# A decoder layer: the feed forward in three bfloat16 planes behind a survey of its weights, and score sets read by two engines

## The chip, the cores and the metric

The kernel runs on one core of a Trainium2 chip. The time is device microseconds of one execution; the lower the better. The number to predict is the median of the timed runs of the changed kernel, to be set beside 1361.11 us, the median of three runs of the kernel before (1361.1 to 1364.54 us).

A core has five engines that matter here, each with its own stream of instructions, executed in order, and semaphores between them: TensorE (PE, with its weight loads shown apart as PEld), VectorE (DVE), ScalarE (ACT), GpSimd (POOL) and SyncE (SP), which issues most of the DMAs. Matmul results land in PSUM, in eight banks of 512 float32 columns by 128 partitions.

## The reference

A decoder layer in float32: causal self-attention, cross-attention to 77 context rows, and a gated feed forward with two further hidden layers, each with a residual and a layer norm behind it. B = 2, T = 1024, C = 256, 16 heads of 16, hidden size 1024.

```python
def _L0_ffn_ref(x, w1_w, w1_s, w2_w, w2_s, h1_w, h1_s, h2_w, h2_s, w3_w, w3_s):
    h = jax.nn.silu(_tlin(x, w1_w, w1_s)) * _tlin(x, w2_w, w2_s)
    h = jax.nn.gelu(_tlin(h, h1_w, h1_s), approximate=False)
    h = jax.nn.gelu(_tlin(h, h2_w, h2_s), approximate=False)
    return _tlin(h, w3_w, w3_s)
...
x = _layernorm(x + _L0_attn_ref(x, L0_attn_w_qkv, L0_attn_w_proj), axis=-1)
x = _layernorm(x + _L0_xattn_ref(x, ctx_1024, ctx_1024, mask, ...), axis=-1)
x = _layernorm(x + _L0_ffn_ref(x, ...), axis=-1)
```

`_tlin(x, w, s)` is `x @ w.T * s`. The five feed-forward matrices hold only -8, 0 and 8 (ternary values times 8); the scales `s` are ordinary float32 vectors. In bfloat16 a weight of -8, 0 or 8 is the same number as in float32.

## The kernel before

The 16 tiles of 128 tokens are worked on in five chunks, `CHUNKS = ((0, 0, 2), (0, 2, 2), (1, 0, 4), (0, 4, 4), (1, 4, 4))`, each (batch, first tile, tiles). For a chunk the stages are, by the names of the code:

- `start` / `project`: transpose the tokens, project to queries, keys and values, rotate, and pad each head to 32 rows (`qk_pads`, two buffers). Keys and values live in blocks of four tiles, `kT` and `v`, from a pool of three.
- `top` / `maxima` (L353): for each query tile and each span of keys, a set of scores for four heads goes into `su`, the one tile of four PSUM banks (`ps_u`, one buffer). VectorE reads the whole set, up to 2048 columns, and reduces it to `part`. The maximum is then written into the query, so that the next stage subtracts it in the matmul itself.
- `weighted` / `values` (L388 to L416): for each group of four heads and each key tile, scores into the same `su`, one exponential by ScalarE over all four banks into `pr` (L400), a triangular mask by GpSimd on the diagonal (L403), and the product with the values into `po` one step later.
- `rest`: `self_finish` (divide, project, residual, norm) and `cross` (the same scheme with the context's keys: maxima at L461, exponentials at L482).
- `fed` / `feed_forward`: from the normalized tokens, transposed in `transposed_tokens`, the gated pair `pg`, `pu` (8 pairs, two matmuls each), two hidden layers `pf` (8 x 8 matmuls each), and the last matrix (8 matmuls a tile). All are float32. Weights come in 22 slices of 128 x 1024, each fetched anew for every chunk by SP into a pool of five (`wffn`).

What sets the order. `run(start(0))`, `top(0)`, `weighted(0)`, `cross_keys()` come first, then `rest(0)` together with `start(1)`. From there `beside(work, filler)` runs: the attention of the chunks 1 to 4 is the work, the feed forward of chunks that have left attention is the filler. Each `yield` of the attention gives a number of microseconds as credit, and so much feed forward is put in; `filling` ties a feed-forward matmul to the attention two steps back (`AHEAD = 2`), so that it does not run further ahead. What is left of the feed forward when the attention ends runs alone (the tail). `alone` marks the last chunk, where the hidden layers' Gelu reads PSUM directly instead of four at a time. Within this the scheduler of the program orders the instructions of each engine.

Most matmuls are issued in two helpers, so in the profile attention's are at L69 and the feed forward's at L83.

Of the kernel before, what the change touches and what calls it, by code (L numbers as in the profile page):

```python
# [10 lines left out]
U8 = mybir.dt.uint8  # L11
AF = mybir.ActivationFunctionType
# [4 lines left out]
P = 128  # L17
# [10 lines left out]
CHUNKS = ((0, 0, 2), (0, 2, 2), (1, 0, 4), (0, 4, 4), (1, 4, 4))  # L28
# [8 lines left out]
def kernel(ctx: ExitStack, tc: tile.TileContext, a: dict, out: bass.AP):  # L37
# [7 lines left out]
    small = pool("small", 4)  # L45
    wself = pool("wself")
    wcross = pool("wcross")
    keys = pool("keys", 3)
    queries = pool("queries", 2)
    work = pool("work", 2)  # L50
    probs = pool("probs", 2)
    ps_u = ctx.enter_context(tc.tile_pool(name="ps_u", bufs=1, space=PSUM))
    ps_o = ctx.enter_context(tc.tile_pool(name="ps_o", bufs=1, space=PSUM))
    ps_f = ctx.enter_context(tc.tile_pool(name="ps_f", bufs=3, space=PSUM))
# [32 lines left out]
    def bank(name="pm"):  # L87
        return ps_f.tile([P, 512], F32, tag="f", name=name)

    def scores_bank(name="su"):  # L90
        return ps_u.tile([P, 4, 512], F32, tag="u", name=name)
# [31 lines left out]
    for i in range(2):  # L123
        pad = wself.tile([P, 2, H, 32], F32, name=f"qk_pad{i}")
        nc.gpsimd.memset(pad, 0.0)
        nc.gpsimd.memset(pad[:, 1, :, D : D + 1], -1.0)
        qk_pads.append(pad)
# [7 lines left out]
    bv = wcross.tile([1, C], F32, name="bv")  # L135
# [5 lines left out]
    maskk = wcross.tile([L, T], BF16, name="maskk")  # L141
    kx = [wcross.tile([P, NG, L], F32, name=f"kx_{b}") for b in range(B)]
# [9 lines left out]
    def cross_keys():  # L152

        with ExitStack() as first:
# [6 lines left out]
            nc.sync.dma_start(wv, a["wvT"].rearrange("(k p) n -> p k n", p=P))  # L161
            for w, name in ((bk, "bk"), (bv, "bv"), (bq, "bq"), (bo, "bo")):
                nc.sync.dma_start(w, a[name])
# [33 lines left out]
    def add_residual(xt, ps, mv):  # L197

        nc.vector.tensor_tensor(xt, ps, xt, ALU.add)
        stats = small.tile([P, 6], F32, tag="stats", name="stats")  # L200
        nc.vector.bn_stats(stats, xt)
        nc.vector.bn_aggr(mv, stats)

    def normalize(tiles, mv):
        rstd = small.tile([P, len(tiles)], F32, tag="rstd", name="rstd")
# [5 lines left out]
    def transposed_tokens(b, t0, n):  # L211

        xT = work.tile([P, KC, n * P], F32, tag="xTc", name="xTc")
# [17 lines left out]
    def attend(osb, i):  # L231
# [5 lines left out]
        rec = small.tile([P, H, 1], F32, tag="rec", name="rec")  # L237
        nc.vector.reciprocal(rec, pov[:, :, D : D + 1])
        y = work.tile([P, C], F32, tag="y", name="y")
# [7 lines left out]
        yT = work.tile([P, KC, P], F32, tag="yT", name="yT")  # L247
# [5 lines left out]


    kT, v = {}, {}

    def project(b, t0, n, q):

        kb = t0 // KT
        if t0 % KT == 0:  # L260
            kT[b, kb] = keys.tile([P, NG, KB], F32, tag="kT", name="kT")
            v[b, kb] = keys.tile([P, KT, H * DV + 16], F32, tag="v", name="v")
            nc.gpsimd.memset(v[b, kb], 1.0)
        for i in range(n):
# [4 lines left out]
            xT = work.tile([P, KC, P], F32, tag="xT", name="xT")  # L269
# [6 lines left out]
            turned = work.tile([P, 2, H, D], F32, tag="turned", name="turned", bufs=1)  # L276
# [8 lines left out]
            pad = qk_pads[i % 2]  # L285
# [9 lines left out]
            nc.scalar.copy(heads_of(v[b, kb][:, t % KT])[:, :, :D], pv[:, :C].rearrange("p (h d) -> p h d", h=H))  # L295
            yield 0.3
            for s, to, at in ((0, q, i), (1, kT[b, kb], t % KT)):
# [22 lines left out]
    def maxima(b, t0, n, q):  # L320

        for i in range(n):
            cols = slice(i * P, (i + 1) * P)
            spans = spans_of(t0 + i)
            part = small.tile([P, len(spans), NG, 4], F32, tag="part", name="part")
            for m, (kk, c0, c1) in enumerate(spans):
# [3 lines left out]
                for g0 in range(0, NG, gs):  # L330
# [8 lines left out]
                    for gi in range(gm):  # L339
                        for j in range(4):  # L340
# [6 lines left out]
                                        kT[b, kk][rows, g0 + gi, c0:c1],  # L347
# [5 lines left out]
                    nc.vector.tensor_reduce(  # L353
                        part[:, m, g0 : g0 + gm, :].rearrange("p g j -> p j g"),
                        su[:, :, : gm * r].rearrange("p j (g r) -> p j g r", g=gm),
                        AX.X,
                        ALU.max,
                    )
                    yield 2.6 * gm * r / KB
# [4 lines left out]
    def values(b, t0, n, q, osb):  # L364

        nk = t0 + n
        for g in range(NG):
            po = ps_o.tile([P, n * P], F32, tag="o", name="po")

            def weigh(k, q0, pr):  # L370
# [4 lines left out]
                            values_of(v[b, k // KT][:, k % KT], 4 * g + j),  # L375
# [8 lines left out]
            for k in range(nk):  # L384
# [7 lines left out]
                            kT[b, k // KT][rows[j], g, k % KT * P : (k % KT + 1) * P],  # L392
# [6 lines left out]
                pr = probs.tile([P, 4, n * P], F32, tag="pr", name="pr")  # L399
                nc.scalar.activation(pr[:, :, q0:], su[:, :, q0 : n * P], AF.Exp)  # L400
# [14 lines left out]
                yield 1.4 * (n * P - q0) / KB  # L415
# [4 lines left out]
    def self_finish(b, t0, n, osb):  # L420
        mv = small.tile([P, n, 2], F32, tag="mv", name="mv")
# [11 lines left out]
    def cross(b, t0, n):  # L433
        x1T = yield from transposed_tokens(b, t0, n)
        qx = queries.tile([P, NG, n * P], F32, tag="q", name="qx")
# [6 lines left out]
        for i in range(n):  # L442
# [7 lines left out]
            for g in range(NG):  # L450
# [9 lines left out]
            top = small.tile([P, NG, 4], F32, tag="top", name="top")  # L460
            nc.vector.tensor_reduce(  # L461
                top.rearrange("p g j -> p j g"),
                su[:, :, : NG * L].rearrange("p j (g l) -> p j g l", g=NG),
                AX.X,
                ALU.max,
            )
# [4 lines left out]
            yield 2.0  # L471
        osb = work.tile([P, NG, n * P], F32, tag="osb", name="osb", bufs=1)
        for g in range(NG):
# [7 lines left out]
            pr = probs.tile([P, 4, n * P], F32, tag="pr", name="pr")  # L481
            nc.scalar.activation(pr[:L], su[:L, :, : n * P], AF.Exp)  # L482
            po = ps_o.tile([P, n * P], F32, tag="o", name="po")
# [8 lines left out]
            yield 1.4 * n / KT  # L492
        mv = small.tile([P, n, 2], F32, tag="mv", name="mv")
# [12 lines left out]
    def feed_forward(b, t0, n, alone):  # L506


        slices = iter(range(N12 + 2 * NH + N3))

        def weights():
            w = wffn.tile([P, SLICE], F32, tag="wf", name="wf")
            nc.sync.dma_start(w, a["wf"][next(slices)])
            return w

        x2T = yield from transposed_tokens(b, t0, n)
        hid = acts.tile([P, FC, n * P], F32, tag="hid", name="hid")
        for f in range(FC):
            if f % 2 == 0:
                w = weights().rearrange("p (f s k n) -> p f s k n", f=2, s=2, k=KC)  # L520
            pg = bank("pg")[:, : n * P]
            for k in range(KC):
                filling(pg, w[:, f % 2, 0, k, :], x2T[:, k, :], start=(k == 0), stop=(k == KC - 1))
            yield 0.43 * n
            pu = bank("pu")[:, : n * P]
            for k in range(KC):
                filling(pu, w[:, f % 2, 1, k, :], x2T[:, k, :], start=(k == 0), stop=(k == KC - 1))

            gate = acts.tile([P, n * P], F32, tag="gate", name="gate", bufs=2)
            nc.scalar.activation(gate, pg, AF.Tanh, scale=sc[:, 0, f : f + 1])  # L530
            nc.vector.scalar_tensor_tensor(gate, gate, 1.0, pg, ALU.add, ALU.mult)
            nc.vector.scalar_tensor_tensor(hid[:, f, :], pu, sc[:, 1, f : f + 1], gate, ALU.mult, ALU.mult)
            yield 0.43 * n
        for s in (2, 3):
            nxt = acts.tile([P, FC, n * P], F32, tag="hid" if s == 3 else "mid", name="nxt")
            for f in range(FC):
                w = weights().rearrange("p (k n) -> p k n", k=FC)
# [5 lines left out]
                if alone:  # L543
# [71 lines left out]
    def top(n):  # L615
        yield from maxima(*CHUNKS[n], q[n])

# [127 lines left out]
```

## Time and profile before

| what | value |
|---|---|
| median of three runs | 1361.11 us |
| the profiled execution | 1359.41 us |
| its span, first to last instruction | 1357.7 us |
| mean granted TensorE clock | 0.932 |
| instructions in the span | 15205 |
| moved by DMA | 66.19 MB, mean 49 GB/s |
| feed-forward weight slices | 110 DMAs of 512 KB, median 3.2 us to landing |

A page's rows of groups give the line, the engine, the operation, what it writes and reads with its shape, the count, then busy us and mean ns of one, then the idle time of the engine just before such instructions and what ended it. A float32 matmul appears as two MATMUL records. Matmuls are pipelined and the record of one spans its way through the array, so the records of a run overlap: the cost of one in a run is the distance from start to start, not its own length. In the timeline a run of equal instructions is merged into one row: start, length from the first start to the last end, and the count.

The page's chain that ended last gives TensorE 82% of the span, ScalarE 7%, VectorE 7%.

### The profile page before, as it was taken

What the parts mean: (1) busy time and instruction counts of PE and PEld (TensorE: products, weight loads), DVE (VectorE), ACT (ScalarE), POOL (GpSimd) and SP (SyncE); (2) the same over time, 40 slices, a digit from 0 to 9 for tenths busy, and PEclk for the clock granted to TensorE, in tenths of its full rate; (3) what the DMA queues carried; (4) which work ended last, traced back from release to release, by engine and by line L of the source; (5) the groups of instructions that cost most, each with busy time, mean ns of one, the idle gap of its engine ahead of it and who ended that gap; (6) DMA issues with size and microseconds to landing.
All of it is one profiled execution on the core that took longest, in us unless ns stands there. A gap on an engine that the chain in (4) does not pass through costs nothing.

```text
span 1357.7 us, 15205 instructions
## 1 busy us (share of the span) xinstructions
PE 1245.1 (92%) x6672; PEld 638.9 (47%) x6672; DVE 455.4 (34%) x705; ACT 304.9 (22%) x328; POOL 84.0 (6%) x131
## 2 busy tenths in 40 slices
PE   6978998898999999998989999899899798999997
PEld 3554646675466755432225544543222343554445
DVE  3133603346133347750003334686000232140002
ACT  1211151211431121004452212010444303011110
POOL 2110011000211000000011000000000000000000
PEclk7585899898899899999999989899899998999999
DMA  5010211122111112110000000111000000122220
GB/s 161 32 47 0 78 48 47 48 78 85 47 61 49 63 47 70 47 63 16 32 31 17 31 31 32 47 47 47 32 31 17 32 26 22 62 92 72 73 74 15
DMA packets 24594, 66.19 MB, mean 49 GB/s; under 512 B 4328, under 2 KB 9553, under 8 KB 24529
## 3 DMA queue, kind: packets, MB, share of 16 engines
q1 hardware_dynamic: 24257, 64.44, 14.3%
q8 instruction: 52, 0.85, 0.3%
q10 hardware_dynamic: 272, 0.79, 0.2%
q14 instruction: 13, 0.11, 0.0%
HBM read 63.12 MB, written 2.10 MB: 48 GB/s over the span
## 4 chain that ended last, share of the span: by engine, by line
PE 82%; ACT 7%; DVE 7%; POOL 2%; issue 2%; DMA 1%; SPq 0%; POOLq 0%; ACTq 0%; DVEq 0%
PE pf L83 36%; PE su L69 18%; PE pm L69 7%; PE po L69 6%; PE pg L83 4%; PE pu L83 4%; ACT pr L400 3%; DVE part L353 2%; PE pq L69 2%; PE pt L226 1%; ACT pr L482 1%; PE pt L235 1%; PE pt L300 1%; DVE top L461 1%; PE pt L246 1%
## 5 line engine op out<-in xcount | busy, mean ns | idle before, releaser
L83 PE MATMUL pf<-nxt,wf 128*128 128x512 f32 (+1 forms) x640 | 251.1, 535 | 0.0
L83 PE MATMUL pf<-hid,wf 128*128 128x512 f32 (+1 forms) x640 | 249.8, 524 | 0.0
L353 DVE TENSOR_REDUCE part<-su 128x4 f32<-128x2048 f32 (+3 forms) x76 | 165.5, 2178 | 76.2 <-PE su L69 75.8
L400 ACT ACTIVATE pr<-su 128x2048 f32<-128x2048 f32 (+1 forms) x104 | 140.6, 1352 | 208.9 <-PE su L69 208.7
L83 PEld LDWEIGHTS pf<-hid,wf 128*128 128x128 f32 x640 | 113.4, 190 | 119.8 <-issue 114.3
L83 PEld LDWEIGHTS pf<-nxt,wf 128*128 128x128 f32 x640 | 122.0, 201 | 98.5 <-issue 91.1
L69 PE MATMUL su<-q,kT 17*128 17x512 f32 (+3 forms) x832 | 97.7, 538 | 26.7 <-ACT pr L400 24.8
L69 PE MATMUL su<-kT,q 16*128 16x128 f32 (+3 forms) x1152 | 92.3, 434 | 12.4 <-DVE part L353 12.1
L546 DVE TENSOR_SCALAR nxt<-pf,sc 128x256 f32<-128x256 f32 (+1 forms) x64 | 39.4, 615 | 181.6 <-PE pf L83 181.0
L69 PE MATMUL po<-pr,v 128*32 128x512 f32 (+3 forms) x832 | 90.5, 510 | 2.0 <-POOL pr L403 1.5
L69 PEld LDWEIGHTS su<-q,kT 17*128 17x128 f32 x832 | 35.6, 197 | 90.1 <-ACT pr L400 59.1
L417 DVE COPY osb<-po 128x512 f32<-128x512 f32 (+1 forms) x20 | 11.7, 585 | 186.7 <-PE po L69 186.7
L403 POOL TENSOR_SCALAR_AFFINE_SELECT pr<-pr 128x512 f32<-128x512 f32 x64 | 40.6, 635 | 513.6 <-ACT pr L400 513.6
L69 PEld LDWEIGHTS su<-kT,q 16*128 16x128 f32 x1152 | 45.7, 205 | 51.9 <-DVE part L353 25.9
L83 PE MATMUL pg<-xTc,wf 128*128 128x512 f32 (+1 forms) x160 | 69.2, 552 | 0.3 <-DVE xTc L218 0.3
L83 PE MATMUL pu<-xTc,wf 128*128 128x512 f32 (+1 forms) x160 | 65.8, 530 | 0.1
L530 ACT ACTIVATE gate<-pg,sc 128x512 f32<-128x512 f32 (+1 forms) x40 | 24.1, 601 | 185.2 <-PE pg L83 185.1
L83 PE MATMUL pf<-wf,nxt 128*128 128x256 f32 x256 | 58.4, 385 | 0.0
L548 ACT ACTIVATE nxt<-nxt 128x1024 f32<-128x1024 f32 (+1 forms) x16 | 23.7, 1483 | 134.1 <-DVE nxt L546 133.9
L83 PEld LDWEIGHTS pf<-wf,nxt 128*128 128x128 f32 x256 | 48.7, 193 | 9.0 <-issue 1.6
L565 DVE TENSOR_TENSOR o<-pf,s 128x256 f32<-128x256 f32 x16 | 6.8, 423 | 134.8 <-PE pf L83 134.8
L482 ACT ACTIVATE pr<-su 77x2048 f32<-77x2048 f32 (+1 forms) x20 | 30.6, 1531 | 64.2 <-PE su L69 64.2
(103 smaller groups left out, 1018.9 us busy)
## 6 DMA issues: line engine op xcount, KB each, us to landing
wf<-in_wf_dram SPq DMA_DIRECT2D x110, 512.0 KB, 3.2
x<-in_x_dram SPq DMA_DIRECT2D x16, 128.0 KB, 3.4
out_dram<-x SPq DMA_DIRECT2D x16, 128.0 KB, 1.8
wqkv<-in_w_qkv_dram ACTq DMA_DIRECT2D x1, 768.0 KB, 4.9
wk<-in_wkT_dram SPq DMA_DIRECT2D x1, 512.0 KB, 5.2
wq<-in_wqT_dram SPq DMA_DIRECT2D x1, 512.0 KB, 3.5
rope<-in_rope_dram SPq DMA_DIRECT2D x1, 256.0 KB, 5.1
wproj<-in_w_proj_dram SPq DMA_DIRECT2D x1, 256.0 KB, 5.0
```

The lines of the kernel that those rows point to most:

```text
L69: latest[0] = nc.tensor.matmul(*args, **kw).ins
L83: ins = nc.tensor.matmul(*args, **kw).ins
L226: nc.tensor.transpose(pt[:, g * P : (g + 1) * P], m_pad[:, 4 * g : 4 * g + 4, :].rearrange("p h d -> p (h d)"), ident)
L235: nc.tensor.transpose(pt[:, g * P : (g + 1) * P], osb[:, g, i * P : (i + 1) * P], ident)
L246: nc.tensor.transpose(pt[:, k * P : (k + 1) * P], y[:, k * P : (k + 1) * P], ident)
L353: nc.vector.tensor_reduce(part[:, m, g0 : g0 + gm, :].rearrange("p g j -> p j g"), su[:, :, : gm * r].rearrange("p j (g r) -> p j g r", g=gm),
L400: nc.scalar.activation(pr[:, :, q0:], su[:, :, q0 : n * P], AF.Exp)
L403: nc.gpsimd.affine_select(out=pr[:, :, q0 : q0 + P], in_=pr[:, :, q0 : q0 + P], compare_op=ALU.is_ge, fill=0.0, base=0, pattern=[[0, 4], [ ...
L482: nc.scalar.activation(pr[:L], su[:L, :, : n * P], AF.Exp)
L530: nc.scalar.activation(gate, pg, AF.Tanh, scale=sc[:, 0, f : f + 1])
L546: nc.vector.tensor_scalar(nxt[:, f, :], pf, sc[:, s, f : f + 1], None, ALU.mult)
L548: nc.scalar.activation(nxt[:, f - 3 : f + 1, :], nxt[:, f - 3 : f + 1, :], AF.Gelu)
```

## The change

1. **A survey and a branch.** While chunk 0 is in attention, `survey` reads the 22 weight slices once. VectorE takes the maximum of the low halves of the 32-bit words, ScalarE copies the high halves as bfloat16, and a DMA writes that copy to `wh` in DRAM. One matmul adds the partitions' maxima up; `flag` is 0 if all low halves are zero. All engines load the flag and branch. `start(0)` is followed by chunk 0's attention, the cross keys, the remaining loads, `rest(0)` and `start(1)` beside the survey; everything from `top(1)` on is built twice, once in each arm.
2. **Three planes.** In the arm for flag 0 the activation is split: `upper` is the high half of the float32 word as bfloat16, the remainder is taken by VectorE, its high half is `mid`, and what is left is stored as bfloat16 in the low halves, `lower`. Each matmul becomes three bfloat16 products, one for each plane, with float32 sums in PSUM. `upper` and `lower` are read in place, at a step of two bfloat16 elements. The other arm is the float32 feed forward.
3. **Two banks each.** In `largest` ScalarE copies banks 2 and 3 of a score set to `aside` while VectorE reduces banks 0 and 1; VectorE then reduces the copy. In `exponentials` VectorE copies banks 2 and 3 to `pr` while ScalarE takes the exponential of banks 0 and 1; ScalarE then does the copied half in place.
4. **Buffers, order, pace.** Keys and values have two fixed blocks, queries two fixed buffers (the cross queries reuse a chunk's own), `qk_pads` one. The chunk (0, 4, 4) comes before (1, 0, 4). Credits: 1.6 instead of 2.6 for a maximum, 0.6 instead of 1.4 for an exponential, 1.3 instead of 2.0 for a cross maximum; a feed-forward step counts 0.215 us a product of 512 columns.

```diff
-CHUNKS = ((0, 0, 2), (0, 2, 2), (1, 0, 4), (0, 4, 4), (1, 4, 4))
+CHUNKS = ((0, 0, 2), (0, 2, 2), (0, 4, 4), (1, 0, 4), (1, 4, 4))
...
+    def largest(to, su):
...
+        nc.scalar.copy(aside, su[:, 2:])
+        nc.vector.tensor_reduce(to[:, :2], su[:, :2], AX.X, ALU.max)
+        nc.vector.tensor_reduce(to[:, 2:], aside, AX.X, ALU.max)
+
+    def exponentials(pr, su):
+
+        nc.vector.tensor_copy(pr[:, 2:], su[:, 2:])
+        nc.scalar.activation(pr[:, :2], su[:, :2], AF.Exp)
+        nc.scalar.activation(pr[:, 2:], pr[:, 2:], AF.Exp)
...
-                    nc.vector.tensor_reduce(
+                    largest(
                         part[:, m, g0 : g0 + gm, :].rearrange("p g j -> p j g"),
                         su[:, :, : gm * r].rearrange("p j (g r) -> p j g r", g=gm),
-                        AX.X,
-                        ALU.max,
                     )
-                    yield 2.6 * gm * r / KB
+                    yield 1.6 * gm * r / KB
...
-                nc.scalar.activation(pr[:, :, q0:], su[:, :, q0 : n * P], AF.Exp)
+                exponentials(pr[:, :, q0:], su[:, :, q0 : n * P])
...
-                yield 1.4 * (n * P - q0) / KB
+                yield 0.6 * (n * P - q0) / KB
...
+    def split(x, mid, k0, k1):
+
+        upper, lower = word_halves(x)
+        left = pl.acts.tile([P, k1 - k0, x.shape[-1]], F32, tag="left", name="left", bufs=2)
+        nc.vector.tensor_tensor(left, x[:, k0:k1, :], upper[:, k0:k1, :], ALU.subtract)
+        left_upper = word_halves(left)[0]
+        nc.scalar.copy(mid[:, k0:k1, :], left_upper)
+        nc.vector.tensor_tensor(lower[:, k0:k1, :], left, left_upper, ALU.subtract)
+
+    def planes_summed(sums, K, step, first):
...
+        if first:
+            early = K // 2 if K > KC else 0
+            runs = [[(p, k) for k in range(early) for p in range(3)]] if early else []
+            runs += [[(p, k) for k in range(early, K)] for p in range(3)]
+        else:
+            runs = [[(p, k) for k in range(K) for p in range(3)]]
...
+                    filling(
+                        ps,
+                        *operands(p, k),
...
+    def survey(flag):
...
+            for i in range(N12 + 2 * NH + N3):
+                w = raw.tile([P, SLICE], F32, tag="w", name="w")
+                nc.sync.dma_start(w, a["wf"][i])
+                low = w.bitcast(U16).rearrange("p (n two) -> p n two", two=2)[..., 0]
+                nc.vector.tensor_reduce(seen[:, i : i + 1], low, AX.X, ALU.max)
+                h = raw.tile([P, SLICE], BF16, tag="h", name="h")
+                nc.scalar.copy(h, w.bitcast(BF16).rearrange("p (n two) -> p n two", two=2)[..., 1])
+                nc.sync.dma_start(wh[i], h)
+                yield 1
...
+    with part():
+        run(start(0))
+        run(together((chain(top(0), weighted(0), cross_keys(), attention()), 1.0), (survey(flag), 0.8)))
+    other_weights = nc.values_load(flag, min_val=0, max_val=1)
...
+    with tc.If(other_weights == 0) as exact:
+        beside_each_other(feed_forward_exact, 5)
+    with exact.Else():
+        beside_each_other(feed_forward, 4)
```

The new `feed_forward_exact` has the loops of `feed_forward`. The first sums of a layer are made in pairs, in the order of `first` above, so that the planes that are ready late are used late; `split` is called for every two blocks of a finished hidden layer.

## The prediction

> **What bounds the kernel now.** I read the page first, then busy time by stretches, then the timeline where one kind of work stands alone, then the waits.
>
> ```profile
> PE 1245.1 (92%) x6672; PEld 638.9 (47%) x6672; DVE 455.4 (34%) x705; ACT 304.9 (22%) x328; POOL 84.0 (6%) x131
> ```
>
> TensorE is busy nearly throughout, the others a third or less. Cutting the span where the kinds of work change (first feed-forward matmul at 142 us, last attention matmul at 1162) gives, with busy us and instruction counts:
>
> ```profile
> 0.00:142.00 142.00, 109.67 (x672) 64.01 (x672) 45.22 (x79) 22.89 (x43) 17.06 (x36) 0.67 0.18 57
> 142.00:1162.00 1020.00, 947.82 (x5499) 479.80 (x5496) 378.06 (x558) 263.64 (x260) 63.13 (x89) 0.96 0.13 44
> 1162.00:1358.00 196.00, 187.61 (x506) 95.06 (x505) 32.15 (x69) 18.41 (x25) 3.77 (x6) 0.99 0.20 67
> ```
>
> Columns after the width: PE, weight load, DVE, ACT, POOL, granted clock, DMA share, GB/s. The opening has no filler: attention of chunk 0 runs as a chain of latencies at clock 0.67. The middle is attention with feed forward between its sets, the tail feed forward alone. In both TensorE is the bound, so what counts is the price of one pass:
>
> ```profile
> 1289.63 6.60 PE L83 MATMUL pf<-nxt,wf 128*128 128x512 f32 x15
> 1290.06 0.19 PEld L83 LDWEIGHTS pf<-nxt,wf 128*128 128x128 f32 x1 [0.24 <-issue]
> 1290.49 0.19 PEld L83 LDWEIGHTS pf<-nxt,wf 128*128 128x128 f32 x1 [0.24 <-issue]
> ```
>
> ```profile
> 1183.32 2.97 PE L83 MATMUL pf<-wf,nxt 128*128 128x256 f32 x13
> ```
>
> ```profile
> 307.50 1.03 PE L69 MATMUL su<-causal,ident_h 128*128 128x512 bf16 x4
> ```
>
> Weight loads start 0.43 us apart, so a float32 pass over 512 columns costs 0.43; the counts (640 records for 320 matmuls) say two passes a matmul, 0.86. At 256 columns (2.97-0.38)/12 = 0.216. The last record of a run carries about 0.38 us of pipeline at these settings, so the four bfloat16 mask passes are (1.03-0.38)/3 = 0.216 apart at 512 columns. Half of 0.216 for 256 is an estimate.
>
> **The feed forward.** Ternary weights times 8 are exact in bfloat16; the activation is cut in three bfloat16 planes. One float32 matmul (two passes, 0.86) becomes three bfloat16 passes (3 x 0.216 = 0.65).
> - Before: 960 passes of 512 (three four-tile chunks, 160 matmuls each) x 0.43 = 413, and 640 + 256 of 256 columns x 0.216 = 193: 606 us.
> - After: 1440 x 0.216 = 311, and 1344 x 0.108 = 145: 456 us. Gain 150, all on TensorE, the bound.
> - Weight loads: 0.10 us in bfloat16 (the ident_h rows), under the 0.216 pass; under the 0.108 passes just covered. If not covered, 1344 x some 0.05 = 67 us lost. I take none: the 256-column bfloat16 mask passes already run with a load each.
>
> No trace row reads bfloat16 at a 4-byte step, as the upper and lower planes are read here. Nearest by type is the 0.216 row; nearest by bytes is the float32 word at 0.43. The Trainium skill ("SBUF — State Buffer", section on the DMA port swizzle, its note on cachelines) says SBUF is read in 16-byte lines, full speed needs two hits per line, and bfloat16 may step up to 8 elements free. A step of 2 hits four times. By that rule 456 us; by the float32 row two planes of three cost double: 480 x 1.076 + 448 x 0.54 = 758. I take 0.216, since operand type sets the passes in every row here.
>
> **The splits.** Per four-tile chunk 13 splits of 1024 elements: two DVE operations and an ACT copy. DVE rows:
>
> ```profile
> L353 DVE TENSOR_REDUCE part<-su 128x4 f32<-128x2048 f32 x32 | 73.2, 2289 | 23.0 <-PE su L69 23.0
> L353 DVE TENSOR_REDUCE part<-su 128x4 f32<-128x1536 f32 x16 | 28.1, 1755 | 14.0 <-PE su L69 13.9
> L400 ACT ACTIVATE pr<-su 128x1024 f32<-128x1024 f32 x28 | 28.6, 1023 | 54.4 <-PE su L69 54.4
> ```
>
> (2289-1755)/512 = 1.04 ns an element, so 1.22 us for 1024. Over four chunk-equivalents 52 x 2.44 = 127 us DVE and 52 x 1.02 = 53 us ACT, beside TensorE while other products run. Uncovered are the layer ends: 3 a chunk, about 2.4 us less what the early planes cover. In the tail I charge 4 us.
>
> **Two banks each.** A 2048-column maximum held the one score set for 2.29 us. After, ACT copies two banks (1.02) while DVE reduces two (1.22), and DVE reduces the copy off the path. The exponential held it 1.88; after, the slower of DVE's copy (1.22) and ACT's exponential (1.02), with the second exponential later on ACT. DVE gains about 107 us of copies and 13 of overhead, ACT about 86 + 21. What could be got back is what TensorE shows as waiting:
>
> ```profile
> PE su L69 <- ACT pr L400: 25.0, 24, 3.9
> PE su L69 <- DVE part L353: 15.4, 9, 4.6
> PE su L69 <- DVE top L461: 10.9, 8, 1.6
> ```
>
> 51 us; most of a release's 2 us was already filled with feed forward, so I take 30. Ends: 0, and 60 if the pipeline ends behind those waits shrink too.
>
> **Order and pace.** Credits for filler fall to 1.6 and 0.6, and chunk (0,4,4) now comes before (1,0,4). In the built program TensorE's list, after the last attention matmul, holds 504 products and then 576: 888 of 512 columns and 192 of 256, 888 x 0.216 + 192 x 0.108 = 213 us. Filler then runs out once: in the rest of chunk 2 and the start of the next maxima the list shows no feed forward over some 40 us of work. The opening is the price of bare attention (110 busy in 142, clock 0.67); I charge 18, ends 5 and 40. DVE in the middle rises from 378 to about 550 of 850 us; where the gated layer meets maxima, DVE needs about 4.9 us for 3.4 of TensorE. About 12.
>
> Slices of 0.25 instead of 0.5 MB change nothing: the DMA share is 0.13 there. One padded query/key buffer instead of two, and two key blocks instead of three, make a projection wait for the last one's transposes (four passes, under 1 us), 16 times; feed forward covers 12 of them, uncovered they cost 12 us, I take none.
>
> **Opening: survey and branch.** 22 slices: 0.5 MB in, 0.25 MB out, one reduce (1.22) and one copy (1.02): 27 us DVE, 22 us ACT, 17.3 MB. The nearest DMA rows:
>
> ```profile
> 0.00:20.00 20.00, 10.13 (x44) 6.21 (x48) 3.89 (x8) 2.89 (x5) 7.55 (x22) 0.82 0.88 263
> 63.00:72.00 9.00, 7.64 (x41) 3.34 (x40) 1.11 (x3) 1.71 (x4) 0.66 (x2) 0.50 0.79 290
> ```
>
> At 290 GB/s that is 60 us, behind the 20 us of other loads: 80 at the earliest. DVE and ACT run in order: a reduce that waits for its slice has attention's work queued behind it, and on SP the stores wait for copies with loads of x and weights behind them. In the built order all surveys precede the first normalization work:
>
> ```profile
> 69.81 0.26 DVE L238 RECIPROCAL rec<-pt 128x16 f32<-128x16 f32 x1 [1.40 <-PE pt L235]
> ```
>
> So the 69.8 moves to about 93 (ends 75 and 125); the 69 us from there to the opening's last normalization (138.3) lose the 6 of chunk 1's maxima that ran inside, which go to the middle. Opening 160. Then every engine loads the flag and branches, TensorE drained. The trace has no branch inside; the nearest row is a DMA landing (1.8 to 3.2 us). "Runtime: NRT & Kernel Launch", section "Instruction fetch mechanics", says a taken branch outside the fetched window stalls for a page fetch and counsels against control flow. By the landing row, load plus one fetch is about 5; by the rule, unpriced, several engines may each pay, estimate 10 from the same rows. The exact body follows in line, so 5: opening 165.
>
> **The sum.** Tail feed forward before: 370 x 0.43 + 128 x 0.216 = 187, as the window shows. So the middle held 606-187 = 419 of it and 601 of attention, waits and switching. After: 601 + (456-213) = 844, plus 6 moved, minus 30, plus 18 and 12: 850. Tail 213 + 9 of ending + 4 = 226. Span 165 + 850 + 226 = 1241. The profiled execution took 1359.41 with a span of 1357.7; 1.7 more gives 1243, to stand beside the median of 1361.11, itself 1.7 above that execution. I say **1243**.
>
> **Rivals.**
> - In-order queues decide. For: DVE near full in maxima, and survey interleaved with attention on DVE, ACT and SP. Against: DVE's mean is 65%. 84 score sets x 0.5 us = 42, plus 20 more in the opening: 1305. Chance 0.24.
> - Strided planes read at the word's rate, the slower side: 758 instead of 456, so 1545. For: no row reads so. Against: the cacheline rule. It decides once a strided 512 pass costs about 0.30 instead of 0.216; there the gain of 118 is gone. Chance 0.07.
> - The branch goes the other way and float32 runs: 1243 + 150 = 1393. The weights are 0 and ±8, whose low halves are zero. Chance 0.01.
> - The pipeline ends shrink too and waits nearly vanish: below 1190. Chance 0.04.
>
> The forecast itself, 0.64, with its own range 1195 to 1285. From the same cases: faster by over 0.3% (about what a measurement can tell from no change) 0.90, same 0.02, slower 0.08. The range 1190 to 1305 leaves out the slower cases, the fast one and part of the queues' case.
>
> **What would show it.** Feed-forward passes 0.216 apart in the tail for all three planes; tail near 226; first feed-forward matmul near 168; TensorE over 90% busy in the middle; the score reader's row at 1.2 instead of 2.29. Passes of the upper and lower planes at 0.3 or more, a survey ending past 125 us, or DVE over 80% busy in the middle would make it wrong.

## The result, and the profile after

The changed kernel takes **1570.53 us** (median of four runs, 1567.27 to 1573.4) beside 1361.11 us (four runs, 1360.2 to 1364.54) for the kernel before: ratio 1.1538, 95% interval 1.1508 to 1.1568. It is 209 us slower. Forecast were 1243 us, in a range of 1190 to 1305. Of two kernels further down, single runs were over 1.5% slower than the fastest of the same kernel (two of four of `split_su`, one of four of `old_order_split`) and are left out of the times.

The page of the changed kernel, busy time of each engine over a span of 1571.7 us:

```profile
PE 1310.6 (83%) x7543; PEld 602.2 (38%) x7602; DVE 722.6 (46%) x1075; ACT 470.0 (30%) x627; POOL 82.3 (5%) x128
```

TensorE's busy time rose by 65 us although the feed forward got cheaper. Busy time by stretches of the changed kernel, cut at the first feed-forward matmul (155 us) and the last attention matmul (1338); the columns are those of the same view of before:

```profile
0.00:155.00 155.00, 106.96 (x606) 60.47 (x607) 69.44 (x115) 51.08 (x83) 15.13 (x34) 0.69 0.46 156
155.00:1338.00 1183.00, 983.87 (x5868) 437.50 (x5907) 554.59 (x833) 368.43 (x491) 62.39 (x88) 0.78 0.06 17
1338.00:1572.00 234.00, 219.77 (x1070) 104.24 (x1088) 98.59 (x130) 50.50 (x54) 4.80 (x6) 0.99 0.17 46
```

Opening (155 us) and tail (234) are near the forecast (165 and 226). The middle takes 1183 us instead of 850, at a granted clock of 0.78 where it had 0.96. Adding up the periods of half clock over the whole span gives 632 us, against 186 before.

Where did it go? I gave each matmul a slot, the time to the next one's start, at most its own recorded length, and called the rest waiting. Before: attention 586 us, feed forward 659, waiting 101. After: attention 766, feed forward 545, waiting 248. So the feed forward did give 114 us, and attention, whose matmuls are the same, took 180 more, with 147 more of waiting.

Most of the 180 is the clock. It is recorded as full or half, nothing between, and a pass takes twice as long at half: in the kernel before, the float32 passes of 256 columns start 0.216 us apart at full clock and 0.427 at half. An estimate can therefore put every slot back to full clock, by counting the part of it that lies in half-clock periods at half. Attention then takes 527 us before and 558 after, the feed forward 636 and 484, and the half clock adds 81 and 268. Of the 214 us between the two profiled executions, the feed forward gave back 152; waiting took 147 more, the half clock 187 more and attention's own products 31 more.

The waits of the changed kernel say what for (waiting instruction, whom it waited for, us in total, times, longest us):

```profile
ACT pr L280 <- DVE pr L279: 303.4, 111, 10.2
...
DVE part L274 <- ACT aside L273: 56.9, 39, 3.2
...
PE su L77 <- DVE part L274: 50.1, 29, 6.4
...
PE su L77 <- ACT pr L280: 46.4, 43, 4.9
```

The first two rows are new: of the two readers of a score set, one waits for the other. ScalarE's exponential waits for VectorE's copy of the *other* two banks, VectorE's reduction for ScalarE's copy. Both halves belong to one tile, `su`, and the built program carries a semaphore wait between its readers (with two tiles, below, it is gone). One step of `weighted` in the timeline of the changed kernel (start, length, what; in brackets the idle time before and what ended it):

```profile
484.77 1.14 PE L77 MATMUL su<-q,kT 17*128 17x512 f32 x8 [0.92 <-ACT pr L280]
485.84 0.16 PEld L77 LDWEIGHTS po<-pr,v 128*32 128x32 f32 x8 [0.76 <-issue]
485.84 1.07 PE L77 MATMUL po<-pr,v 128*32 128x512 f32 x8
486.05 1.22 DVE L279 COPY pr<-su 128x1024 f32<-128x1024 f32 x1 [2.39 <-PE su L77]
...
486.84 0.29 PE L91 MATMUL pf<-hid,wf 128*128 128x256 bf16 x1
486.97 0.27 PE L91 MATMUL pf<-hidm,wf 128*128 128x256 bf16 x1
487.31 1.02 ACT L280 ACTIVATE pr<-su 128x1024 f32<-128x1024 f32 x1 [1.64 <-DVE pr L279]
...
488.38 0.93 PE L77 MATMUL su<-q,kT 17*128 17x384 f32 x8 [1.15 <-ACT pr L280]
```

VectorE reads from 486.05 to 487.27, ScalarE only then, and the next scores start at 488.38: the set is held 2.33 us, not 1.22, and longer than the 1.88 of the single exponential before. Beside it stand two feed-forward passes of 0.11 us, and TensorE waits 1.15 us.

### The profile page after: what moved, and what is told of

It reads as the page before. It is cut to its first block, busy times and chain, and to the rows that moved or that the text cites. A ratio compares the mean times of both kernels' runs of the same rounds, so it can differ in the third digit from the quotient of the medians.

```text
span 1571.7 us, 17857 instructions
## 1 busy us (share of the span) xinstructions
PE 1310.6 (83%) x7543; PEld 602.2 (38%) x7602; DVE 722.6 (46%) x1075; ACT 470.0 (30%) x627; POOL 82.3 (5%) x128
## 5 line engine op out<-in xcount | busy, mean ns | idle before, releaser
L91 PEld LDWEIGHTS <-wf 128*128 128x128 bf16 x2400 | 236.3, 103 | 316.7 <-issue 148.4
L279 DVE COPY pr<-su 128x1024 f32<-128x1024 f32 (+3 forms) x124 | 113.3, 914 | 251.9 <-PE su L77 249.4
L280 ACT ACTIVATE pr<-su 128x1024 f32<-128x1024 f32 (+3 forms) x124 | 96.1, 775 | 305.9 <-DVE pr L279 303.4
L91 PE MATMUL pf<-hid,wf 128*128 128x512 bf16 (+1 forms) x630 | 178.4, 367 | 1.6 <-issue 0.5
L91 PE MATMUL pf<-mid,wf 128*128 128x512 bf16 (+1 forms) x629 | 174.9, 364 | 1.9 <-issue 1.6
L274 DVE TENSOR_REDUCE part<-su 128x2 f32<-128x1024 f32 (+3 forms) x76 | 88.6, 1165 | 57.1 <-ACT aside L273 56.9
L91 PE MATMUL pf<-hidm,wf 128*128 128x512 bf16 (+1 forms) x312 | 107.8, 363 | 0.7 <-issue 0.6
L91 PE MATMUL pf<-midm,wf 128*128 128x512 bf16 (+1 forms) x309 | 104.7, 357 | 1.8 <-issue 1.6
L281 ACT ACTIVATE pr<-pr 128x1024 f32<-128x1024 f32 (+3 forms) x124 | 99.2, 800 | 0.0
L275 DVE TENSOR_REDUCE part<-aside 128x2 f32<-128x1024 f32 (+3 forms) x76 | 87.7, 1153 | 0.0
```

Source lines behind the costliest of these rows:

```text
L91: ins = nc.tensor.matmul(*args, **kw).ins
L274: nc.vector.tensor_reduce(to[:, :2], su[:, :2], AX.X, ALU.max)
L275: nc.vector.tensor_reduce(to[:, 2:], aside, AX.X, ALU.max)
L279: nc.vector.tensor_copy(pr[:, 2:], su[:, 2:])
L280: nc.scalar.activation(pr[:, :2], su[:, :2], AF.Exp)
L281: nc.scalar.activation(pr[:, 2:], pr[:, 2:], AF.Exp)
```

## The experiments

The expectations name theories by letters; "serial theory" is S. **S**: the loss is the two readers waiting for each other. **P**: it is the pace, too little filler for the lower credits. **O**: it is the new chunk order with its tighter buffers. Later **C**: attention is a chain of latencies through the one score set, and the feed forward is its cover; against it **PB**: TensorE is the bound and the price of passes counts. "Broken sets" and "fragments" are row-tiled sets pulled apart: four products that each use other rows of the array and run at the same time when they stand together. Times are medians; ratios are to the kernel before on the same chip, with 95% intervals.

### One reader, one pace, one split at a time

`split_su` makes the score set two tiles of two banks, so that the readers have no tile in common:

```diff
-        return pl.ps_u.tile([P, 4, 512], F32, tag="u", name=name)
+        return [pl.ps_u.tile([P, 2, 512], F32, tag=f"u{h}", name=f"{name}{h}") for h in range(2)]
```

> The score set is two tiles of two banks each instead of one tile of four, so the built program no longer makes the second reader wait for the first; credits, chunk order and everything else as in the changed kernel. Theory S (the two readers of a set run one after the other, which holds the set 2.2 to 2.6 us instead of about 1.3): 216 sets about 1 us shorter, so the middle falls by some 200 us and the time to about 1350. Theory P (the credits of 1.6, 0.6 and 1.3 leave too little feed forward between the sets, TensorE idles and its granted clock is halved): the filler stays thin, so no less than 1500. Theory O (chunk (0,4,4) second runs out of filler): no less than 1480.

`one_reader` goes back to a single reader (`tensor_reduce(to, su)`, `activation(pr, su, AF.Exp)`) and the old credits; `one_reader_low` keeps the low credits; `credits_back` keeps both readers and takes the old credits:

```diff
-                    yield 1.6 * gm * r / KB
+                    yield 2.6 * gm * r / KB
...
-                yield 0.6 * (n * P - q0) / KB
+                yield 1.4 * (n * P - q0) / KB
...
-            yield 1.3
+            yield 2.0
...
```

> One reader for the whole set as before (one reduce, one exponential) and the credits of before (2.6, 1.4, 2.0); survey, branch, three planes and chunk order as in the changed kernel. S and P both expect the middle near what was predicted, 1230 to 1300, with the granted clock back over 0.9; O expects a bare stretch that stays, 1350 or more.

> One reader for the whole set, but the changed kernel's credits (1.6, 0.6, 1.3). S: holds of 2.29 and 1.88 instead of about 2.55 and 2.25, so 216 x 0.3 = 70 us less, about 1500. P: as slow as the changed kernel, within 2% of 1570, clock near 0.8.

> The changed kernel with the credits of before (2.6, 1.4, 2.0), the two readers in series left as they are. P: 1350 or less and the clock over 0.9. S: the sets are still held 2.2 to 2.6 us; feed forward fills more of it, about 1450 to 1500.

| run | us | ratio |
|---|---|---|
| split_su | 1441.48 (1438.97 and 1443.98) | none on record |
| one_reader | 1369.61 | 1.0046 (1.0020 to 1.0071) |
| one_reader_low | 1413.27 | 1.0397 (1.0345 to 1.0450) |
| credits_back | 1493.44 | 1.0958 (1.0911 to 1.1006) |

With the old credits, going from two readers to one gives 1493 - 1370 = 124 us; with the low ones 1571 - 1413 = 157. The low credits cost 1571 - 1493 = 77 us with two readers and 44 with one. So S is the larger part and P real. But `one_reader` came out at 1370 where both expected 1230 to 1300, in the region that only O had named, and `one_reader_low` at 1413 below both S (1500) and P (1570): neither sized the rest of the loss. `credits_back` lies where S put it. `split_su` missed S's 1350 too. In its timeline the readers do run together,

```profile
484.55 1.02 ACT L280 ACTIVATE pr<-su 128x1024 f32<-128x1024 f32 x1 [0.53 <-PE su L77]
484.62 1.23 DVE L279 COPY pr<-su 128x1024 f32<-128x1024 f32 x1 [1.68 <-PE su L77]
```

0.07 us apart and at the durations they have alone. That gains 129 us over the change, yet the time is 91 us above S's. The Trainium skill ("PSUM — Partial Sum Buffer", PSUM bank collisions raise a hardware error) has it that two engines may read different banks at the same time; these rows agree. The wait in the changed kernel was the program's, made from the tile, not the chip's. Why the split stays behind the kernel before is taken up below.

### The old order, and single parts put into the kernel before

`old_order_one` and `old_order_split` add to `one_reader` and `split_su` the old chunk order, three key blocks, one buffer each for `left` and `gate`, and three weight slices. `before_banks` puts the two readers of the change, and nothing else, into the kernel before; `before_order` only the chunk order:

```diff
-CHUNKS = ((0, 0, 2), (0, 2, 2), (1, 0, 4), (0, 4, 4), (1, 4, 4))
+CHUNKS = ((0, 0, 2), (0, 2, 2), (0, 4, 4), (1, 0, 4), (1, 4, 4))
```

> As the run with one reader and the credits of before, but with the chunks in the order of before ((1,0,4) ahead of (0,4,4)) and three key blocks for it (one buffer instead of two for left and gate, three weight slices instead of five, to make room). Theory O (with (0,4,4) second there is no feed forward to fill with for two stretches of 92 and 106 us, which run at half clock): both stretches go, 1240 to 1280, clock over 0.9. If the order doesn't matter: 1370 as without it.

> As the run with the set in two tiles (readers side by side), with the order of before; credits of the changed kernel. S and O together: 1456 less some 150, about 1300 or less. P alone would keep it over 1420, since the credits stay low.

> The kernel before with only the two readers of a score set (one tile of four banks), its credits and order kept. S: a set is held 0.25 to 0.4 us longer, under filler that was just enough: 1380 to 1440. If the two readers did run side by side: 1361 or less.

> The kernel before with only the changed order of chunks. O: its two small chunks hold 152 us of feed forward for the attention of (0,2,2) and (0,4,4), the rest of it runs bare at half clock: 1420 to 1480. If the order doesn't matter: within 1% of 1361.

| run | us | ratio |
|---|---|---|
| old_order_one | 1360.27 | 1.0005 (0.9989 to 1.0020) |
| old_order_split | 1431.42 | 1.0512 (1.0442 to 1.0582) |
| before_banks | 1514.47 | 1.1133 (1.1097 to 1.1169) |
| before_order | 1403.35 | 1.0311 (1.0278 to 1.0343) |

The two readers alone make the kernel before 154 us slower, more than was expected (1380 to 1440). By counts, 76 maxima held 2.55 instead of 2.29 us and 124 exponentials 2.3 instead of 1.88 are 76 x 0.26 + 124 x 0.42 = 72 us. The order costs 44 us in the kernel before, less than O's 59 to 119, and only about 10 (1370 to 1360, with the buffers) with cheap feed forward: O is small. And three planes with one reader and the old order gave nothing at all (1360, where O expected 1240 to 1280), although the feed forward's slots at full clock fall by 153 us. That speaks against PB, and needed a run of its own. `old_order_split` missed the 1300 of S and O together by 131 us.

### Attention without feed forward

`before_noff` is the kernel before without the feed forward: it writes the tokens after cross-attention. `banks_noff` is `before_banks` cut in the same way.

```diff
-        slices = iter(range(N12 + 2 * NH + N3))
...
+        yield 0.1
         for i in range(n):
+            nc.sync.dma_start(out[b, (t0 + i) * P : (t0 + i + 1) * P, :], xs[b][t0 + i])
```

> The kernel before with the whole feed forward left out: the tokens after cross-attention are written as the output. PB (the prediction's view: TensorE is the bound of the middle, so taking passes away shortens it): 142 + 601 + 10, about 760. Theory C (attention is one chain of sets through one score tile, matmul, reader, matmul, reader, and feed forward only fills its waits): the middle hardly falls, 1000 or more, at half clock most of the time.

> The kernel before with the two readers of a score set, and without the feed forward (it writes the tokens after cross-attention). It prices the chain through the one score tile with no filler in it; to be set beside 1148 us for the same with single readers. Serial theory: 76 maxima hold the set 2.55 instead of 2.29 us and 124 exponentials 2.3 instead of 1.88, so 76 x 0.26 + 124 x 0.42 = 72 us more, and the second copies and reductions delay the next step a little: 1200 to 1270 us. Broken-sets theory (the loss of 154 us comes mainly from row-tiled products broken up by full-array masks): the sets are broken less without filler, so at most 1190 us. If the readers did work together, the set would be held shorter and it would be below 1140.

`before_noff` takes 1147.97 us (ratio 0.8433, 0.8393 to 0.8472): leaving out 606 us of TensorE passes saves 213. C expected 1000 or more, at half clock most of the time; PB's 760 is far off. But **1148 us is attention alone at a granted clock of 0.62**. Its middle:

```profile
142.00:1147.00 1005.00, 737.25 (x4120) 305.36 (x4112) 290.94 (x393) 196.75 (x192) 61.27 (x85) 0.61 0.01 2
```

876 us lie in half-clock periods. By slots, attention's products take 519 us at full clock, as before, 290 us are waiting (101 before), and the half clock adds 326 (81 before). So the run shows two things that the feed forward covered: waiting, and the loss of the clock. It doesn't show that attention needs 1148 us; at full clock its slots and waits would be 809.

One step of that chain with nothing beside it, timeline of `before_noff`:

```profile
629.88 1.88 ACT L400 ACTIVATE pr<-su 128x2048 f32<-128x2048 f32 x1 [1.06 <-PE su L69]
631.81 0.31 PEld L69 LDWEIGHTS su<-q,kT 17*128 17x128 f32 x8 [1.97 <-ACT pr L400]
631.81 1.14 PE L69 MATMUL su<-q,kT 17*128 17x512 f32 x8 [1.06 <-ACT pr L400]
...
633.08 1.88 ACT L400 ACTIVATE pr<-su 128x2048 f32<-128x2048 f32 x1 [1.32 <-PE su L69]
```

The step is 3.20 us: 1.88 of reading, 0.05 to the next scores, 1.27 until the set is full. That is the floor of such a step with one reader, and the kernel before was above it, with TensorE busy throughout:

```profile
993.86 1.06 PE L69 MATMUL po<-pr,v 128*32 128x512 f32 x8
994.06 1.88 ACT L400 ACTIVATE pr<-su 128x2048 f32<-128x2048 f32 x1 [2.10 <-PE su L69]
994.86 1.98 PE L83 MATMUL pf<-hid,wf 128*128 128x512 f32 x4
...
996.77 1.14 PE L69 MATMUL su<-q,kT 17*128 17x512 f32 x8
...
998.04 1.88 ACT L400 ACTIVATE pr<-su 128x2048 f32<-128x2048 f32 x1 [2.10 <-PE su L69]
```

3.98 us. So in these steps TensorE was the bound before, and cheaper filler can take them from 3.98 to 3.20 and no further. The same step in `banks_noff`:

```profile
723.65 1.23 DVE L270 COPY pr<-su 128x1024 f32<-128x1024 f32 x1 [3.33 <-PE su L69]
724.91 1.02 ACT L271 ACTIVATE pr<-su 128x1024 f32<-128x1024 f32 x1 [2.59 <-DVE pr L270]
...
725.99 2.09 PE L69 MATMUL su<-q,kT 17*128 17x512 f32 x8 [0.61 <-ACT pr L271]
...
728.21 1.22 DVE L270 COPY pr<-su 128x1024 f32<-128x1024 f32 x1 [3.34 <-PE su L69]
```

4.56 us. The hold grew from 1.93 to 2.34, and the matmuls that fill the set take 2.09 instead of 1.14 us, since the clock is at half. Of 32 such full steps in each, `before_noff` has 17 near 3.2 us and 14 near 4.15 (same hold, half clock), `banks_noff` 30 near 4.56 and none faster. `banks_noff` takes 1317.83 us (0.9697, 0.9670 to 0.9724), 170 more than with one reader and above every expectation (1200 to 1270 the nearest), with 1143 us of half clock against 876. By slots, 44 of the 170 are waiting, 32 attention's products and 97 the half clock.

### Half by half, and the amount of filler

`halves` (from the change) and `halves_before` (from the kernel before) split the set into two tiles but leave each to its one old reader, a half at a time, without copies. `one_reader_75` is `old_order_one` with credits of 1.95, 1.05 and 1.5: three quarters of the old ones, as 456 us of feed forward are of 606.

```diff
+        for h in range(2):
+            nc.scalar.activation(pr[:, 2 * h : 2 * h + 2], su[h], AF.Exp)
```

> The changed kernel with the score set in two tiles of two banks, both read by the engine that read it before the change: VectorE reduces each half, ScalarE takes the exponential of each half; no copies, so TensorE can refill one half while the other is read. Credits and order of the changed kernel. C: the chain step falls from matmuls plus readers to the readers alone, 216 sets x 1 to 1.3 us, 1300 or less. S alone (only the waiting of one reader for the other costs): no better than the run with both readers side by side, 1456.

> The kernel before with only the score set in two tiles read by one engine half by half. C: 1361 less 40 to 100 us. PB: TensorE's passes are the same, within 2% of 1361.

> As the run with one reader and the old order of chunks, with the credits scaled by the price of the new passes (1.95, 1.05 and 1.5, about 0.75 of before), so that the filler lasts to the end of each chunk. PB: 1240 to 1260. C: the sets take as long as before with thinner filler, middle 1000 or more, 1290 to 1340.

| run | us | ratio |
|---|---|---|
| halves | 1490.86 | 1.0966 (1.0899 to 1.1034) |
| halves_before | 1524.16 | 1.1211 (1.1157 to 1.1266) |
| one_reader_75 | 1339.88 | 0.9859 (0.9819 to 0.9899) |

The halves were a plain miss of C, and `halves_before` of PB too: a set released in halves should shorten the chain, and cost 163 us instead. The waits did shrink, from 101 to 82 us in `halves_before`. But attention's slots grew from 586 to 745 us: 72 of that is half clock, and 87 stay at full clock. Sets are broken: the built order alternates between the halves and puts mask products between them. The row of `po<-pr,vx` (the cross-attention's product with the values) shows the same in the two-reader kernels. By shape, kernel before:

```profile
L69 PE MATMUL po<-pr,vx 77*32 77x512 f32 x96 | 12.8, 605 | 4.3 <-ACT pr L482 3.9
```

and the changed kernel:

```profile
L77 PE MATMUL po<-pr,vx 77*32 77x512 f32 x96 | 55.5, 983 | 18.7 <-ACT pr L280 18.7
```

The same 96 records are busy for 12.8 and 55.5 us. Half clock is part of that; at full clock the slots of all `po<-pr,vx` grow from 16 to 40 us. In the built order of the change such a set of four stands as two, two mask products, one, a mask product, one.

`one_reader_75` is the first version that beats the kernel before, at the upper end of what C expected: the filler is spread so that it lasts, and the half clock falls from 401 us (`old_order_one`) to 305. Waiting stays as it was (168 and 167 us), so the gain over `old_order_one` is the clock's. Its full steps are near the chain's floor, 3.28 us, and the next scores' weights wait for the reader:

```profile
1017.31 1.88 ACT L271 ACTIVATE pr<-su 128x2048 f32<-128x2048 f32 x1 [1.40 <-PE su L78]
...
1019.31 0.31 PEld L78 LDWEIGHTS su<-q,kT 17*128 17x128 f32 x8 [0.44 <-ACT pr L271]
1019.31 1.14 PE L78 MATMUL su<-q,kT 17*128 17x512 f32 x8
...
1020.58 1.88 ACT L271 ACTIVATE pr<-su 128x2048 f32<-128x2048 f32 x1 [1.39 <-PE su L78]
```

### Whole sets

`banks_whole` and `after_whole` are `before_banks` and the changed kernel with each row-tiled set ordered behind the one before it:

```diff
                 first = matmul(*args, **kw)
+                if last_of_set[0] is not None:
+                    behind(first, last_of_set[0], "sets stay whole")
...
+        last_of_set[0] = latest[0]
```

> The kernel before with the two readers of a score set, as in the run of 1514 us, and with every row-tiled set of products ordered behind the end of the set before it, so that the cross-attention's products with the values are no longer broken up by the mask products of the next set. Broken-sets theory: those products go back from some 58 to some 17 us start to start, so 1514 - 40 = 1475 us or less. Serial theory (the whole loss lies in the set being held longer): no change, 1500 to 1530, since the broken products lie in time that TensorE would wait anyway.

> The changed kernel, with every row-tiled set of products ordered behind the end of the set before it. Broken-sets theory: 1570 - 40 to 1570 - 55, so 1515 to 1530 us. Serial theory: 1555 to 1580 us; the sum of the half clock periods stays near 630 us.

`banks_whole` takes 1487.86 us (1.0976, 1.0931 to 1.1021) and `after_whole` 1538.4 (1.1311, 1.1269 to 1.1353): 27 and 32 us better. Both theories expected wrongly: the broken sets cost something, but less than the 40 that was expected of them, and 127 of the 154 us stay with the two readers: by slots 52 of waiting, 65 of half clock and 10 of products. The half clock of `after_whole` stays at 612 us.

### Everything together

`split_whole_75` is `old_order_split` with whole sets and the credits of `one_reader_75`; `one_reader_85` has 2.2, 1.2 and 1.7.

> Everything that the runs found, with the change's idea kept: score sets as two tiles of two banks so that the two readers don't wait for each other, row-tiled sets ordered behind one another, the old chunk order, and filler credits of 1.95, 1.05 and 1.5. Chain theory (what the set's hold costs is the cause, and two readers that really run together shorten it from 1.88 to some 1.25 us): below the 1340 us of the single reader with the same order and credits, 1280 to 1330. Fragment theory (two half sets with a mask between break up the row-tiled products, and DVE's extra copies delay the feed forward): above 1360, about 1380 to 1430.

> The three planes and the survey with the single reader and the old chunk order, as in the run of 1340 us, with filler credits of 2.2, 1.2 and 1.7 instead of 1.95, 1.05 and 1.5. More filler beside each set keeps the clock up early and runs out sooner: if thin filler is what costs at 1340 us (305 us at half clock), 1320 to 1335; if running out costs, between 1340 and the 1360 us of credits 2.6, 1.4 and 2.0.

`split_whole_75` takes 1400.65 us (1.0313, 1.0290 to 1.0336), `one_reader_85` 1337.55 (0.9850, 0.9798 to 0.9901). Two readers that really run together are still 61 us behind the single one, as the fragment theory had it. By slots TensorE waits 19 us less than in `one_reader_75`, so the extra copies of VectorE and ScalarE cost no waiting on balance. But attention's products take 58 us more at full clock, and the half clock adds 38. The score sets, filled in two halves, and `po<-pr,vx` make up nearly all of the 58: the records of the latter are busy for 38.3 us against 15.6. The pace is flat between 0.75 and 0.85 of the old one: the two can't be told apart. Busy time of `one_reader_75` in its middle, first feed-forward to last attention matmul:

```profile
148.00:1181.00 1033.00, 909.19 (x6276) 434.68 (x6273) 476.47 (x665) 310.41 (x316) 64.04 (x90) 0.90 0.08 23
```

The middle is still 1033 us long, 13 more than before: waiting there is 124 us instead of 72 and the half clock adds 87 instead of 41, which eats what the cheaper filler gave. The gain is in the tail, 153 us instead of 196.

### Products, waits and clock, run by run

The slots of the main runs, us of the profiled execution. The two columns of products are at full clock; the last one is what the half clock adds to them. The rest of a span lies ahead of TensorE's first product and behind its last.

| run | attention | feed forward | waiting | half clock adds |
|---|---|---|---|---|
| before | 527 | 636 | 101 | 81 |
| the change | 558 | 484 | 248 | 268 |
| before_banks | 561 | 635 | 139 | 167 |
| banks_whole | 537 | 634 | 153 | 146 |
| halves_before | 615 | 635 | 82 | 180 |
| split_su | 606 | 484 | 128 | 211 |
| split_whole_75 | 586 | 483 | 148 | 166 |
| old_order_one | 530 | 483 | 168 | 162 |
| one_reader_75 | 528 | 497 | 167 | 128 |
| before_noff | 519 | 0 | 290 | 326 |

The estimate bears itself out: in the eight kernels with one reader on a whole set, attention's products come to 519 to 532 us, whatever the clock did. What the table can't say is what takes the clock away. Waiting alone doesn't: `halves_before` waits less than the kernel before and loses more than twice as much to the half clock.

## Why the prediction was wrong

The step that failed is the first: "In both TensorE is the bound, so what counts is the price of one pass." For the tail it is true, for the middle only as long as the filler covers the chain of score sets. The middle's sum therefore kept 601 us of attention, waits and switching as they were, let all else come to +6 (-30, 18, 12, and 6 moved from the opening), and had no term for the clock. Measured by slots, the middle's feed forward fell by 185 us (forecast 176), but waiting rose by 127, the half clock by 190 and attention's products by 31: 348 us in place of the 6.

TensorE at 93% of the middle was score sets with feed forward put into their gaps, enough of it to hide the waits and to keep the clock at 0.96. The run without feed forward shows what it hid. It doesn't show that 850 was out of reach: at full clock, attention's slots and waits in its middle come to 709 us. What is shown is that no version with cheaper filler kept the clock (0.93 on the mean before, 0.88 at best with the single reader and three quarters of the credits), and that 153 us of cheaper passes bought nothing at the old pace (`old_order_one`: 67 us more waiting, 81 more from the clock). Why the clock goes stays open. The view that misled was busy time: a gap that is filled with other work doesn't show as a wait. The prediction even had the sign before it, the opening as "a chain of latencies at clock 0.67", and took it for a thing of the opening.

**Two banks each** was the second failure: "the slower of DVE's copy (1.22) and ACT's exponential (1.02)". They ran one after the other, 2.33 us. A gain of 30 us was summed, with no loss among the ends; alone in the kernel before it costs 154: by slots 38 of waiting, 33 of broken sets, 86 of half clock. The prediction named each engine's work on its own banks and never asked whether the program lets both start.

**Order and pace**: 18 us charged for running out of filler, ends 5 and 40. The low credits cost 77 us with two readers, 44 with one; the order 44 in the kernel before and about 10 in the version with one reader.

**Right**: the three planes' passes. In the timeline of the changed kernel's tail, 512 columns:

```profile
1399.80 0.38 PE L91 MATMUL pf<-midm,wf 128*128 128x512 bf16 x1
1400.01 0.61 PE L91 MATMUL pf<-mid,wf 128*128 128x512 bf16 x2
1400.47 0.38 PE L91 MATMUL pf<-midm,wf 128*128 128x512 bf16 x1
```

Three passes in 0.67 us against 0.65 forecast. The two planes read in place take 0.225 each start to start, the plane without step 0.215; with 256 columns 0.114 and 0.108. The rule on cachelines that was weighed holds but for 5%, and the rival in which these planes go at word rate is false: that its 1545 us lie so near the result is chance. Right too were the opening with survey and branch (155 us, forecast 165), the tail (234, forecast 226), and VectorE's load in the middle (554.6 us, forecast about 550). None of the rivals held the true mechanism, and 0.08 for slower was much too little.

## What to carry to other kernels

Before pricing a cheaper filler, leave it out and time the rest. If the rest takes most of the time, the filler was cover, and what counts is how long each resource of the chain is held. Read that run with its clock, though: of the 1148 us here, the half clock makes up 326, where it was 81 with the filler. Slots put back to full clock tell the two apart. Two engines gain nothing on one tile unless the built program lets both start; read its waits, and look whether the split leaves together the products that must run together. When filler gets cheaper, its pace has to fall by about that much: here three quarters of the old credits turned nothing gained (1360 us) into 1.4% (1340 us).

## What the runs showed of the hardware

- The granted clock has two levels here, and one loop runs at either: the exponential step of `before_noff` takes 3.20 or 4.15 us, with the same instructions. In `banks_noff` it stayed at half from 466 to 810 us. The Trainium skill ("TensorE: Matmul & The Clock Gate", A second HAM failure mode: psum-queue depth-cycling) describes short idles between groups that make the clock swing. Waiting alone isn't it in these rows. In the full-clock step of 3.20 us TensorE waits 1.06. In a half-clock step of the same kernel it waits 0.19 of 4.15, and the clock still stays at half for another 10 us. Whether it matters that these products use 17 of 128 rows wasn't tried.

```profile
609.83 2.09 PE L69 MATMUL su<-q,kT 17*128 17x512 f32 x8 [0.47 <-ACT pr L400]
...
613.98 2.09 PE L69 MATMUL su<-q,kT 17*128 17x512 f32 x8 [0.19 <-ACT pr L400]
```

- A pass at half clock takes twice as long: 0.427 instead of 0.216 us for a float32 pass of 256 columns.
- A bfloat16 operand at a step of two costs 0.225 instead of 0.215 us for 512 columns.
- Sets of row-tiled products lose their overlap when a product over all rows comes between them: at full clock the slots of `po<-pr,vx` are 40 us in the change, 24 with the sets kept whole and 16 in the kernel before. Keeping them whole gained 27 and 32 us.
